# The first unit's maxima moved up, and the high parts of q and k stored from ScalarE's queue

## Chip, cores and metric

The kernel runs on one core of one Trainium2 chip. The metric is the device time of one execution in microseconds (us); lower is better.

## What is computed

The reference is a "macaron" layer on x of shape (8, 1024, 256): half a mixture-of-experts step, causal attention with 16 heads of 16, and again half a mixture-of-experts step.

```
x = x + 0.5 * ffn(layernorm(x))     # 8 experts, top 2, capacity 1.25 * N / 8
x = x + attn(layernorm(x))
x = x + 0.5 * ffn(layernorm(x))

attn: q, k, v = x @ Wq.T + bq, split(x @ Wkv.T + bkv)
      dots = causal(q * 16**-0.5 @ k.T);  out = softmax(dots) @ v @ Wo.T + bo
ffn:  probs = softmax(x @ gate_w.T); top 2 experts per token
      keep = counts <= cap     # an expert with more tokens than cap contributes nothing
```

An expert step adds something only where an expert's count stays within the capacity. The kernel computes the gates of both steps beside the attention, counts the tokens, and runs the expert part only if some expert is kept. In the profiled execution none is, so what is timed is the attention with the gates.

## The kernel before

Attention works through 8 batches of 1024 tokens; a batch has four units of four heads, 32 units in all (u = 4b + g). A unit has two streams of 18 tiles each on TensorE:

- **Maxima** (`m_steps`): tiles sm of scores q by k, causally masked, each reduced by VectorE to row maxima (`mx`). After the tiles of a half of the rows, `settle` joins them (`mxr`), makes the negative in a high and a low part (`mneg`), transposes it (`mside`) and has `send` write it to DRAM (`rows`) and read it back in another layout (`neg`).
- **Exponents** (`e_steps`): tiles sc, which begin with the negated maxima taken from `neg` by a matmul with the constant `take_m`; ScalarE takes the exponential (`pT`), GpSimd masks it where the diagonal crosses, and TensorE multiplies it with the values (`pav`).

Both streams share three pairs of PSUM banks: tile n needs the pair of tile n - 3, which its reader (VectorE for sm, ScalarE for sc) must have finished. The stream of maxima runs one unit ahead of that of exponents. Between these tiles, after every third, `gap` takes steps of other work from the queue `work`, at a pace `rate`: for the next batch the transposes (`enter`, pta to xnT), the projections (`project`, pq), the values (`values_of`, pv), and for the last batch the output projection (`leave`, px). Small pieces of VectorE's and GpSimd's work come from the queue `side` (`prepare` and `normed` for the layer norms, `gate_first` for the first step's gates, `biased_late` for adding the output bias to x). `start` sets off sequences of transfers with lags counted in tiles (`fetch`, `send`, `divide`).

`project` makes q and k of eight heads for 512 tokens at a time, eight steps per batch. ScalarE moves the product from PSUM (`whole`), casts it (`high`), and GpSimd takes the difference (`low`); four DMAs of 256 KB store the two parts to DRAM tile `parts`, for q in the order high, low, high, low and for k high, high, low, low. `fetch` reads them back as `qk` with heads along the partitions. Every engine's order is that of the source: each instruction is tied to the one before it on its engine. All these transfers are issued by SyncE (SP); ScalarE issues only loads at the start.

Before the loop over units stands the start: loads, the norm of batch 0 (`prepare_first`, `normed`), weights (`weights`, a generator called `turning`, whose last product is pt_b), projection of the first eight heads, the values of batch 0, the norm of batch 1, memsets and two `fetch`. Then, at u = -1, come the maxima of the first unit alone, and the loop. The profile gives most instructions the line of the helper that records them (L626), so tile names tell them apart.

Of the kernel before, what the change touches and what calls it, by code (L numbers as in the profile page):

```python
# [10 lines left out]
F32 = mybir.dt.float32  # L11
# [9 lines left out]
P = 128  # L21
# [8 lines left out]
def macaron_kernel(  # L30
# [16 lines left out]
    nc = tc.nc  # L47
# [81 lines left out]
                base=-(64 * h + k), channel_multiplier=1,  # L129
            )  # L130
    take_m = const.tile([P, P], F32R, name="take_m")
    nc.vector.tensor_copy(take_m, rows.to_broadcast([P, P]))

    wqT = const.tile([P, DC, D], F32, name="wqT")
    wkT = const.tile([P, DC, D], F32, name="wkT")
# [466 lines left out]
    def attention(run_no, src, dst, gate0, logits, tally):  # L602
# [4 lines left out]
        with stack:  # L607
# [76 lines left out]
            def normed(b, jj):  # L684
                mv, ve, rstd = lns[b]
                for j in (2 * jj, 2 * jj + 1):
                    xn = xns[b, j] = norm.tile([P, D], F32, tag="xn", name=f"xn_a{b}_{j}", bufs=4)
                    ln_apply(xn, xbs[b], j, mv, rstd[:, j : j + 1])
                    yield
                if b:  # L690
                    biased(b, jj)

            coming = {}
# [28 lines left out]
            def prepare_first():  # L722
                st, mv = ln_tiles("a0", "a")
                ve = norm.tile([P, TB], F32, tag="vea", name="ve_a0")
                rstd = norm.tile([P, TB], F32, tag="rstda", name="rstd_a0")
                lns[0] = (mv, ve, rstd)
                for n in (slice(0, TB // 2), slice(TB // 2, TB)):
                    for j in range(TB)[n]:
                        ln_stats(xbs[0], j, st, mv)
                    on.gpsimd.tensor_scalar(ve[:, n], mv[:, n, 1], EPS, None, ALU.add)  # L730
                    on.gpsimd.tensor_tensor(rstd[:, n], ve[:, n], half[:, n], ALU.pow)

            def enter(b):
                xnT = xnTs[b] = ap.tile([P, DC, S], F32, tag="xnT", name=f"xnT{b}", bufs=1)
# [22 lines left out]
            def project(b, gp):  # L757
                xnT = xnTs[b]
                parts = parts_d[b, gp] = passing.tile([2, 8, 4, HD, S], F32, tag=f"parts{gp}", name=f"parts{b}_{gp}")
                for s0 in range(0, S, 512):  # L760
                    for t, (wT, bT, scale) in enumerate(((wqT, bqT, QSCALE), (wkT, bkT, 1.0))):
                        pq = bank(f"pq{b}_{gp}_{s0}_{t}")
                        for o in (0, 256):
                            for c in range(DC):
                                product(
                                    pq[:, o : o + 256],
                                    wT[:, c, gp * P : (gp + 1) * P],
                                    xnT[:, c, s0 + o : s0 + o + 256],
                                    start=(c == 0),
                                    stop=(c == DC - 1),  # L770
                                )
                                if (c, o) != (DC - 1, 256):
                                    yield
                        whole = ap.tile([P, 512], F32, tag="whole", name=f"whole{b}_{gp}_{s0}_{t}")
                        high = ap.tile([P, 512], F32R, tag="high", name=f"high{b}_{gp}_{s0}_{t}", bufs=3)
                        low = ap.tile([P, 512], F32R, tag="low", name=f"low{b}_{gp}_{s0}_{t}", bufs=3)
                        on.scalar.activation(whole, pq, AF.Identity, bias=bT[:, gp : gp + 1], scale=scale)
                        on.scalar.copy(high, whole)
                        on.gpsimd.tensor_tensor(low.bitcast(F32), whole, high.bitcast(F32), ALU.subtract)
                        for c in range(4):  # L780
                            part = (high, low)[c // 2 if t else c % 2]
                            on.sync.dma_start(out=parts[t, :, c, :, s0 : s0 + 512], in_=part.bitcast(F32))
                        yield True


# [62 lines left out]
            def m_steps(u):  # L848
# [56 lines left out]
                def settle(hf):  # L905
                    mx = ap.tile([P, 4, 2, 2], F32, tag="mxr", name=f"mxr{u}_{hf}")
                    on.vector.tensor_reduce(
                        mx.rearrange("p x b a -> p x a b"),
                        mx_tiles[u % 3][hf].rearrange("p h r (a b) s -> p (h r) a b s", a=2),
                        AX.X,  # L910
                        ALU.max,
                    )
                    yield
                    mx = mx.rearrange("p x b a -> p x (b a)")
                    neg = ap.tile([P, 4, 2, 4], F32R, tag="mneg", name=f"mneg{u}_{hf}")
                    high, low = neg[:, :, 0], neg[:, :, 1]
                    on.vector.tensor_scalar(high, mx, -1.0, None, ALU.mult)
                    yield
                    on.vector.scalar_tensor_tensor(
                        low.bitcast(F32), mx, -1.0, high.bitcast(F32), ALU.mult, ALU.subtract  # L920
                    )
                    yield
                    turned = ap.tile([P, 32], F32, tag="mside", name=f"mside{u}_{hf}")
                    on.vector.transpose(turned, neg.bitcast(F32).rearrange("p x c i -> p (x c i)"))
                    start(send(hf, turned), 0)
                    yield

                def send(hf, turned):
                    rows = passing.tile([8, 512], F32, tag="rows", name=f"rows{u}_{hf}")
                    on.sync.dma_start(out=rows.rearrange("c (i s q) -> s c i q", i=4, s=4), in_=turned)  # L930
                    yield 6
                    for h in range(2):
                        on.sync.dma_start(
                            out=negs[u % 2][hf][64 * h : 64 * h + 2, :, :512].bitcast(F32),
                            in_=rows[4 * h : 4 * h + 4].rearrange("(r c) s -> c r s", c=2),
                        )
# [271 lines left out]
            next(turning, None)  # L1208
            next(turning, None)
            drain(read(1))  # L1210
            for t in (vaugs[0], *mx_tiles[0]):
                on.gpsimd.memset(t, 1.0 if t is vaugs[0] else -3.0e38)
            prepare_first()
            for jj in range(2):
                drain(normed(0, jj))
            next(turning, None)
            entering = enter(0)
            next(entering)
            next(entering)
            for jj in range(2, 4):  # L1220
                drain(normed(0, jj))
            projecting = project(0, 0)
            for _ in range(8):
                next(projecting)
            drain(fetch(0, 0, 512))
            drain(entering)
            drain(projecting)
            drain(fetch(0, 512, 512))
            drain(turning)
            drain(values_of(0))  # L1230
            drain(prepare(1))
            for t in (vaugs[1], *mx_tiles[1], *mx_tiles[2]):
                on.gpsimd.memset(t, 1.0 if t is vaugs[1] else -3.0e38)
            for pair_of in negs:
                for t in pair_of:
                    on.gpsimd.memset(t.bitcast(F32), 0.0)
            drain(fetch(1))

            work = deque([project(0, 1)])
            side += [biased_late(0), gate_first(0)]  # L1240
            timed = []
            behind = [0.0]
            last_on = []
# [41 lines left out]
            def maxima():  # L1285
                v, k = divmod(stream[0], 18)
                if v == NU:
                    return
                if k == 0:
                    units[v] = m_steps(v)  # L1290
                steps, settle, done = units[v]
                steps[k]()
                if k == max(done, 8) or k == 17:
                    side.appendleft(settle(int(k == 17)))
                    urgent[0] = 4
                if k == 17:
                    units.pop(v)
                stream[0] += 1

            for u in range(-1, NU):  # L1300
                b, g = divmod(u, NG)
                rate, every = 17 / 12, FILLS
                if u < 0:
                    pass
                elif g == 0:
                    spare[0] = False
                    if b + 1 < B:
# [1 line left out]
                        if b:  # L1309
                            work.append(mixed(leave(b - 1), project(b + 1, 1)))  # L1310
                        else:
                            work.append(project(b + 1, 1))
                        work.append(values_of(b + 1))
                    if b:
                        start(divide(b - 1, 1, 0), 4)
                        after[u - 1, 1] = divide(b - 1, 1, 1)
                        side.append(gate_first(b))
                elif g == 1 and b + 1 == B:
                    work.append(leave(b - 1))
                elif g == 2:  # L1320
                    if b == 0:
                        start(read(2), 40)
# [14 lines left out]
                    start(fetch(u + 2, lag=6), 8)  # L1337
                if u < 0:
                    for n in range(18):
                        step(maxima, 2, 4 if n < 5 else 4 / 3, 1)  # L1340
                else:
                    if u == 0:
                        for n in range(3):
# [86 lines left out]
```

## Time and profile before

| | |
|---|---|
| time, median of 3 runs | 1207.94 us (1207.55 to 1210.71) |
| the profiled execution: its time, its span | 1207.5 us, 1205.5 us |
| busy: PE, DVE, ACT, POOL | 1138.4, 935.2, 735.6, 433.8 us |
| exponentials `pT` | 576 of 1022 ns |
| reductions `mx` | 576 of 1215 ns |
| `high` casts | 64 of 619 ns (median) |
| stores of `parts`, high and low | 128 and 128 of 256 KB, all from SP |
| granted TensorE clock, mean | 0.978 |

PE is TensorE, DVE VectorE, ACT ScalarE, POOL GpSimd, SP SyncE; SPq and ACTq are the issuing of DMAs by these engines, which is not counted as busy time. The span is from the first to the last instruction; the time holds a little more.

### The profile page before, as it was taken

How to read it: one execution, taken by the hardware profiler on the slowest of the kernel's cores; microseconds unless marked ns; L12 is line 12 of the kernel's file. 1: busy time of each engine (PE TensorE's matmuls, PEld its weight loads, DVE VectorE, ACT ScalarE, POOL GpSimd, SP SyncE). 2: the span in 40 equal slices, each digit the busy share in tenths (PEclk: the TensorE clock that was granted, in tenths of full speed). 3: DMA queues.
4: the chain of work that ended last, by engine and by line, in shares of the span. 5: the costliest groups of instructions: out<-in, count | busy, mean ns of one | idle time of the engine just before them, and what ended most of it. 6: DMA issues, size and time to landing. Idle time of an engine off the chain costs nothing.

```text
span 1205.5 us, 36314 instructions
## 1 busy us (share of the span) xinstructions
PE 1138.4 (94%) x15178; PEld 663.1 (55%) x15178; DVE 935.2 (78%) x1652; ACT 735.6 (61%) x955; POOL 433.8 (36%) x772
## 2 busy tenths in 40 slices
PE   6789899999999999999999999999999999999983
PEld 4445555655556555655556555565556555555542
DVE  2687558887788877988788877888789888798834
ACT  3236656766666666665666656566666666665671
POOL 4633313543333423532235433333235322232331
PEclk9879999999999999999999999999999999999997
DMA  5644654354554646455563645546564555543211
GB/s 178 222 168 141 209 173 128 111 196 153 171 185 154 198 159 190 143 172 177 157 201 113 207 153 168 169 155 202 160 181 150 176 174 177 155 136 109 63 42 39
DMA packets 108517, 190.25 MB, mean 158 GB/s; under 512 B 24752, under 2 KB 42296, under 8 KB 108344
## 3 DMA queue, kind: packets, MB, share of 16 engines
q1 hardware_dynamic: 104952, 185.59, 47.8%
q8 instruction: 122, 2.00, 0.7%
q10 hardware_dynamic: 3392, 2.24, 0.6%
q14 instruction: 51, 0.42, 0.1%
HBM read 94.50 MB, written 93.31 MB: 156 GB/s over the span
## 4 chain that ended last, share of the span: by engine, by line
PE 76%; DVE 13%; DMA 5%; issue 1%; ACT 1%; POOL 1%; SPq 1%; POOLq 0%; ACTq 0%; DVEq 0%
PE sc L626 22%; PE pav L626 21%; PE sm L626 15%; PE pq L626 8%; DVE mx L626 8%; PE px L626 4%; PE pv L626 4%; PE pta L626 2%; DVE st_a L626 1%; DMA few<-sums 1%; DMA neg<-rows 1%; DMA rows<-mside 1%; SPq L626 1%; DVE mv_a L626 1%; DMA qk<-parts 1%
## 5 line engine op out<-in xcount | busy, mean ns | idle before, releaser
L626 DVE TENSOR_REDUCE mx<-sm 128x2 f32<-128x1024 f32 (+2 forms) x576 | 684.7, 1215 | 161.6 <-PE sm L626 159.9
L626 ACT ACTIVATE pT<-sc 128x1024 f32<-128x1024 f32 x576 | 573.0, 1022 | 309.6 <-PE sc L626 297.9
L626 PE MATMUL pav<-pT,vaug 128*32 128x256 f32 (+3 forms) x4608 | 329.7, 387 | 2.0 <-ACT att L626 1.4
L626 POOL TENSOR_SCALAR_AFFINE_SELECT pT<-pT 128x256 f32<-128x256 f32 (+1 forms) x448 | 191.0, 443 | 297.2 <-ACT pT L626 290.4
L626 PE MATMUL sm<-qk 64*128 64x512 f32 (+3 forms) x1536 | 266.2, 384 | 17.4 <-DVE mx L626 8.4
L626 PE MATMUL sc<-neg,take_m 64*128 64x512 f32 x1152 | 263.7, 454 | 16.6 <-DVE mx L626 8.9
L626 PE MATMUL sc<-qk 64*128 64x512 f32 (+3 forms) x1536 | 228.7, 334 | 0.0
L626 PEld LDWEIGHTS sm<-qk 64*128 64x128 f32 x1536 | 140.7, 187 | 120.4 <-issue 51.9
L626 POOL TENSOR_TENSOR low<-whole,high 128x512 f32<-128x512 f32 x64 | 82.0, 1282 | 311.3 <-ACT high L626 302.5
L626 PEld LDWEIGHTS pav<-pT,vaug 128*32 128x32 f32 x4608 | 113.7, 109 | 108.0 <-issue 52.2
L626 PEld LDWEIGHTS sc<-neg,take_m 64*128 64x128 f32 x1152 | 109.4, 186 | 106.8 <-issue 53.6
L626 PEld LDWEIGHTS sc<-qk 64*128 64x128 f32 x1536 | 146.2, 186 | 16.3
L626 PE MATMUL sm<-masked,before_k 64*128 64x128 bf16 (+1 forms) x1280 | 86.3, 213 | 0.0
L626 PE MATMUL pq<-xnT,wqT 128*32 128x256 f32 x1024 | 76.3, 391 | 0.5 <-ACT xnT L626 0.5
L626 PE MATMUL px<-woT,on 128*32 128x264 f32 x1024 | 76.5, 387 | 0.2 <-ACT on L626 0.2
L626 PE MATMUL pq<-xnT,wkT 128*32 128x256 f32 x1024 | 73.2, 395 | 0.0
L626 PE MATMUL pv<-wvT,xnT 128*32 128x264 f32 x1024 | 72.3, 390 | 0.0
L626 PEld LDWEIGHTS <-before_k 64*128 64x128 bf16 x1280 | 37.9, 96 | 43.1 <-issue 26.6
L626 POOL TENSOR_TENSOR x_a<-x_a,bo_all 128x512 f32<-128x512 f32 x32 | 41.6, 1304 | 28.1 <-DVE xn_a L626 28.1
L626 PEld LDWEIGHTS pq<-xnT,wqT 128*32 128x32 f32 x1024 | 34.0, 112 | 31.8 <-issue 13.9
L626 DVE TENSOR_TENSOR x_a<-px,x_a 128x256 f32<-128x256 f32 x64 | 26.2, 410 | 31.2 <-PE px L626 30.6
L626 PEld LDWEIGHTS px<-woT,on 128*32 128x32 f32 x1024 | 34.7, 110 | 26.6 <-issue 9.8
(131 smaller groups left out, 741.4 us busy)
## 6 DMA issues: line engine op xcount, KB each, us to landing
qk<-parts SPq DMA_DIRECT2D x124, 512.0 KB
parts<-high SPq DMA_DIRECT2D x128, 256.0 KB
parts<-low SPq DMA_DIRECT2D x128, 256.0 KB
sums<-att SPq DMA_DIRECT2D x62, 256.0 KB
out_dram<-x_a SPq DMA_DIRECT2D x16, 512.0 KB
on<-sums SPq DMA_DIRECT2D x30, 256.0 KB
rs<-inv SPq DMA_DIRECT2D x30, 256.0 KB
x_a<-in_L_attn_x_dram SPq DMA_DIRECT2D x13, 512.0 KB
```

Source lines behind the costliest of these rows:

```text
L626: i = call(*args, **kwargs)
```

## The change

Four things change. (1) In `project`, the DMAs of the high part are issued by ScalarE, behind the cast, in every batch; only the first store of q and of k in the whole kernel stays with SyncE. The low parts stay with SyncE. (2) For unit 0, `send` issues from ScalarE's queue, with other lags, and its first half is settled right after its fifth tile. (3) The start is put in another order: the norm of batch 0 is made in pieces of two, two and four tiles, the statistics of batch 1 come before the rest of the weights, and the values of batch 0 move from ahead of the loop into the work between the first unit's maxima; the gates and biases of batches 0 and 1 move into the loop. (4) In batch 0 the pace is 13/12 instead of 17/12, and the values of batch 1 are mixed with the second projection.

```
     prepare_first:
+        def some(j0, j1): ln_stats for j0..j1, then ve and rstd on GpSimd
+        memset vaugs[0], mx_tiles[0]
+        some(0, 2); some(2, 4)
+        drain(normed(0, 0)); next(turning, None); drain(normed(0, 1))
+        on.vector.tensor_copy(take_m, rows.to_broadcast([P, P]))
+        some(4, 8)
     project:
-        on.sync.dma_start(out=parts[t, :, c, :, s0 : s0 + 512], in_=part.bitcast(F32))
+        queue = on.scalar if part is high and (b or gp or s0 or c) else on.sync
+        queue.dma_start(out=parts[t, :, c, :, s0 : s0 + 512], in_=part.bitcast(F32))
     settle, send:
-        start(send(hf, turned), 0)
+        start(send(hf, turned), 0 if u else 2)
+        queue = on.sync if u else on.scalar      # rows and neg
-        yield 6
+        yield 6 if u else 4
     the start:
         projecting, fetch(0, 0, 512)
+        drain(normed(0, 2)), drain(normed(0, 3))
         drain(entering); drain(projecting); drain(fetch(0, 512, 512))
+        drain(fetch(1))
+        preparing = prepare(1); its first TB + 1 steps
+        memsets of negs, mx_tiles[1], mx_tiles[2], vaugs[1]
         drain(turning)
-        drain(values_of(0)); drain(prepare(1)); memsets; drain(fetch(1))
-        work = deque([project(0, 1)])
-        side += [biased_late(0), gate_first(0)]
+        work = deque([values_of(0), project(0, 1)])
+        side.append(preparing)
     maxima:
-        if k == max(done, 8) or k == 17:
+        if k == (max(done, 8) if v else done) or k == 17:
     the loop:
-        rate, every = 17 / 12, FILLS
+        rate, every = (17 if b else 13) / 12, FILLS
         g == 0, b == 0:
-            work.append(project(b + 1, 1)); work.append(values_of(b + 1))
+            work.append(mixed(values_of(b + 1), project(b + 1, 1)))
+            side.append(gate_first(0)); side.append(biased_late(0))
         g == 1, b == 0:
+            side.append(biased_late(1))
         u < 0:
-            step(maxima, 2, 4 if n < 5 else 4 / 3, 1)
+            step(maxima, 1, 16 / 5 if n < 5 else 16 / 13, 1)
```

More of the change, by code (lines that the diff above doesn't have):

```diff
@@ L131, in macaron_kernel @@
     take_m = const.tile([P, P], F32R, name="take_m")
-    nc.vector.tensor_copy(take_m, rows.to_broadcast([P, P]))
     wqT = const.tile([P, DC, D], F32, name="wqT")
@@ L689, in normed @@
                     yield
-                if b:
+                if b > 1:
                     biased(b, jj)
@@ L726, in prepare_first, with some @@
                 lns[0] = (mv, ve, rstd)
-                for n in (slice(0, TB // 2), slice(TB // 2, TB)):
-                    for j in range(TB)[n]:
+                def some(j0, j1):
+                    for j in range(j0, j1):
                         ln_stats(xbs[0], j, st, mv)
+                    n = slice(j0, j1)
                     on.gpsimd.tensor_scalar(ve[:, n], mv[:, n, 1], EPS, None, ALU.add)
                     on.gpsimd.tensor_tensor(rstd[:, n], ve[:, n], half[:, n], ALU.pow)
+                for t in (vaugs[0], *mx_tiles[0]):
+                    on.gpsimd.memset(t, 1.0 if t is vaugs[0] else -3.0e38)
+                some(0, 2)
+                some(2, 4)
+                drain(normed(0, 0))
+                next(turning, None)
+                drain(normed(0, 1))
+                on.vector.tensor_copy(take_m, rows.to_broadcast([P, P]))
+                some(4, 8)
             def enter(b):
@@ L924, in settle @@
                     on.vector.transpose(turned, neg.bitcast(F32).rearrange("p x c i -> p (x c i)"))
-                    start(send(hf, turned), 0)
+                    start(send(hf, turned), 0 if u else 2)
                     yield
                 def send(hf, turned):
+                    queue = on.sync if u else on.scalar
                     rows = passing.tile([8, 512], F32, tag="rows", name=f"rows{u}_{hf}")
-                    on.sync.dma_start(out=rows.rearrange("c (i s q) -> s c i q", i=4, s=4), in_=turned)
-                    yield 6
+                    queue.dma_start(out=rows.rearrange("c (i s q) -> s c i q", i=4, s=4), in_=turned)
+                    yield 6 if u else 4
                     for h in range(2):
-                        on.sync.dma_start(
+                        queue.dma_start(
                             out=negs[u % 2][hf][64 * h : 64 * h + 2, :, :512].bitcast(F32),
@@ L1210, in attention @@
             drain(read(1))
-            for t in (vaugs[0], *mx_tiles[0]):
-                on.gpsimd.memset(t, 1.0 if t is vaugs[0] else -3.0e38)
             prepare_first()
-            for jj in range(2):
-                drain(normed(0, jj))
-            next(turning, None)
             entering = enter(0)
@@ L1219, in attention @@
             next(entering)
-            for jj in range(2, 4):
-                drain(normed(0, jj))
             projecting = project(0, 0)
@@ L1225, in attention @@
             drain(fetch(0, 0, 512))
+            for jj in range(2, 4):
+                drain(normed(0, jj))
             drain(entering)
@@ L1228, in attention @@
             drain(fetch(0, 512, 512))
-            drain(turning)
[L1230 to L1237, printed above, removed]
-            work = deque([project(0, 1)])
-            side += [biased_late(0), gate_first(0)]
+            drain(fetch(1))
+            preparing = prepare(1)
+            for _ in range(TB + 1):
+                next(preparing)
+            for k in range(2):
+                for t in negs[k]:
+                    on.gpsimd.memset(t.bitcast(F32), 0.0)
+                for t in mx_tiles[k + 1]:
+                    on.gpsimd.memset(t, -3.0e38)
+            on.gpsimd.memset(vaugs[1], 1.0)
+            drain(turning)
+            work = deque([values_of(0), project(0, 1)])
+            side.append(preparing)
             timed = []
@@ L1311, in attention @@
                         else:
-                            work.append(project(b + 1, 1))
-                        work.append(values_of(b + 1))
+                            work.append(mixed(values_of(b + 1), project(b + 1, 1)))
+                        if b:
+                            work.append(values_of(b + 1))
                     if b:
@@ L1316, in attention @@
                         after[u - 1, 1] = divide(b - 1, 1, 1)
-                        side.append(gate_first(b))
+                    side.append(gate_first(b))
+                    if not b:
+                        side.append(biased_late(b))
                 elif g == 1 and b + 1 == B:
                     work.append(leave(b - 1))
+                elif g == 1 and b == 0:
+                    side.append(biased_late(1))
                 elif g == 2:
```

## The prediction

> **What bounds the kernel now.** I read the page first: its busy line and the chain that ended last.
>
> ```profile
> PE 1138.4 (94%) x15178; PEld 663.1 (55%) x15178; DVE 935.2 (78%) x1652; ACT 735.6 (61%) x955; POOL 433.8 (36%) x772
> PE 76%; DVE 13%; DMA 5%; issue 1%; ACT 1%; POOL 1%; SPq 1%; POOLq 0%; ACTq 0%; DVEq 0%
> ```
>
> TensorE is 94% busy and carries 76% of the chain; ScalarE carries 1%, so what it does now is nearly all covered. An average hides stages, so next come the stretches (length, busy time of PE, PEld, DVE, ACT, POOL, then granted clock, DMA share, GB/s):
>
> ```profile
> 34.00:46.20 12.20, 9.53 (x164) 5.05 (x156) 5.43 (x18) 4.83 (x18) 4.18 (x6) 1.00 0.61 211
> 46.20:76.50 30.30, 22.62 (x211) 10.26 (x211) 28.77 (x39) 4.75 (x8) 17.91 (x18) 0.72 0.60 217
> 147.00:153.00 6.00, 0.24 (x5) 0.16 (x2) 0.93 (x1) 1.02 (x1) 1.05 (x3) 0.72 0.50 178
> 261.00:406.00 145.00, 144.09 (x1987) 84.32 (x1980) 118.58 (x202) 95.37 (x125) 56.40 (x99) 1.00 0.54 171
> ```
>
> There are three regimes. Up to 76.5 us VectorE is the limit once its reductions begin (28.77 of 30.30 us). At 147 us everything stands still for 5.8 us. From 261 us on TensorE works 99% of the time, so each microsecond in which it waits is added to the total. The chain in order of time, before 77 us, gives the landmarks:
>
> ```profile
> 32.27 7.95 PE pv L626 x128
> 43.92 2.33 DVE xn_a L626 x4
> 46.24 1.14 DVE mx L626
> 71.36 4.99 DMA neg<-rows
> 76.49 0.84 PE sc L626 x4
> ```
>
> The value product of batch 0 is on the path for 8 us, then the normalising of batch 1; the first reduction starts at 46.2 and the first score tile at 76.5, after a DMA.
>
> **Part 1, the first unit's maxima move up (a gain).** In the changed order the maxima's first products follow pt_b directly, the value product is threaded between them, and VectorE's statistics of batch 1 come before it waits for pt_b.
> - pt_b ends at 32.27 now. ScalarE must also issue stores between its casts there. Two issues of 0.58 us each (row below) after the third cast push the next chain by about 1.2 us and the last pair adds as much, less the 0.78 us that this cast now waits for an older store: 1.8 us net. pt_b ends at 34.1 and the first reduction starts at 35.0, not 46.2.
> - The first five products (about 0.75 us each) now have all 16 value steps between them (128 matmuls took 7.95 us, so 0.45 to 0.5 each): 3.8 + 7.2 = 11 us, so the fifth reduction ends near 46. VectorE normalises three of batch 1's four tiles (0.64 us each) inside that.
> - Then the first half is settled (mxr, two mneg at 1.2 and mside: 2.8 us, as at 59.1 to 61.9 now), 13 reductions at 1.21 make 15.7, one tile 0.6, the second settling 1.2, one reduction of the next unit 1.2: 46 + 21.5 = 67.5. The score tile starts at 67.5 instead of 76.5: 9.0 us.
> - The gating of batch 0 (lc_f 1.17 us and some eight pieces of 0.2) leaves this stretch for the first attention unit, where VectorE is busy about 70%, and costs nothing there; without that cover it is some 4 us. The bias additions of batches 0 and 1 on GpSimd (8 of 1.3 us) go where it was busy 24 of 70 us: nothing. The memsets (neg 4.5 us for four, vaug 2.0) stay ahead of their first use.
> - The first unit's rows and neg copies go to ScalarE's queue. The second neg copy waits for the landing of rows (3.8 us after its issue ended, at 78.3 to 82.1 now), and behind it stands the second exp: 1.5 us back, between 0 and 3.
> Together 7.5 us gained. Bounds: 4 if the qk loads (now 42.95 to 52.3) arrive too late for the sixth product, 12 if PE's half clock (0.72 in the stretch) also goes.
>
> **Part 2, the standstill at 147 us (a gain).** The fourth qk load is issued at 143.28 behind a neg copy that waited 6.5 us for rows and behind four stores; TensorE stands before an sm until 152.87. The profile names no releaser there ("issue", 5.75 us); I infer this load, the only input of that tile still on its way. The pace of projection in batch 0 falls from 17/12 to 13/12, so the stores spread out, and half of them leave SP's queue. Between 0 and 8 us (5.8 and some half clock after it); I take 6, as later batches, with wider spacing, show no such wait.
>
> **Part 3, the high stores on ScalarE's queue (a loss).** Cost of one issue, from the tile view of high, and one place in the timeline:
>
> ```profile
> L626 SPq DMA_DIRECT2D parts<-high x128: 565/582/1683, 17.7 to 1029.7; - x128
> ```
> ```profile
> 253.90 0.69 ACT L626 ACTIVATE whole<-pq,bqT 128x512 f32<-128x512 f32 x1 [0.92 <-POOL pT L626]
> 254.04 0.40 PE L626 MATMUL sc<-neg,take_m 64*128 64x512 f32 x2
> 254.62 0.62 ACT L626 CAST high<-whole 128x512 fp32r<-128x512 f32 x1
> 255.15 2.18 ACT L626 ACTIVATE pT<-sc 128x1024 f32<-128x1024 f32 x2
> 256.22 0.56 PE L626 MATMUL sm<-qk 64*128 64x128 f32 x4
> ```
>
> Now the exp starts 0.1 us before the cast's end. With two stores in between, the queue waits for the cast (0.1 plus 0.02 to 0.07), issues twice (pairs take 1.23 us on SP) and starts the exp: 1.40 us later. Behind these issues stand the exps, and behind an exp stands TensorE: three PSUM pairs are shared by sm and sc, so the second sm after an sc needs that sc's exp done. Here sc (254.04) is read by the exp that ends at about 256.2 and sm starts at 256.22: no slack, so the whole 1.40 is lost. I read the slack so for the eight places of one batch (casts at 239.4, 245.5, 254.6, 262.5, 279.6, 294.1, 311.5, 328.1), letting ScalarE's idle time work the delay off and taking the worst exp of each. What is left over at 1.40 is 0.45, 0.47, 1.42, 0.47, 0.02, 0.64, 0.53, 0.21: 4.2 us. Six such batches make 25.3, the batch at 96 to 160 makes 4.4 in the same way: 29.7. The curve is steep: a delay of 1.0 leaves 11, 1.2 leaves 20, 1.6 leaves 41, 2.0 leaves 63. TensorE is idle some 11 of 839 us from 261 to 1100 for VectorE's sake and a little falls in there: I take 27.
>
> What SP gains for it: 126 issues of mean 0.65, but in the queue's own waits it stands most for ScalarE's cast (135.9 us, 48 times), that is, it has time; a qk load is waited for by sm only 1.9 us in all. No gain after batch 0.
>
> The Trainium skill, DMA: Bandwidth & Descriptors, section "Issuing engines are not separate DMA queues", speaks against the split: issuing from several engines saves only the sequencer's issue time, which is usually small beside the DMA. By it parts 2 and 3 would bring no transport at all, and the sum without part 2 would be 6 us longer. The trace agrees for the steady batches and leaves batch 0 open, where the pace, not the queue, is my reason.
>
> **The sum.** 27 - 7.5 - 6 = +13.5 us, against the profiled execution's 1207.5 us (span 1205.5 and 2.0 around it; the median is 0.4 higher): 1221, and I give 1220. With the ends of each part for a delay of 1.2 to 1.6 (17 to 38), the forecast's own range is 1209 to 1233.
>
> **The rivals.**
> - Faster: the issues find cover. The path is the exp behind the cast, at 56 places; it decides at a delay of about 1.1 us, below which the loss (under 15) is less than the 13.5 gained. For it: the chain has ScalarE at 1%, and ScalarE idles 470 us. Against it: the slack above is 0 to 1.5 us and the two shortest issues already take 1.13. At 1.0 it is 11 - 12 - 6 = -7: 1200. Chance 0.18.
> - Slower by far: an issue on ScalarE takes what SP's fourth of a burst takes (low stores reach a mean of 0.86 us and a maximum of 1.9), or its store waits for the landing of an older DMA on the other queue, which it now can. At a delay of 1.9 (57) less 13.5: 1251. For it: SP and ScalarE now issue at the same time. Against it: high stores come first in their burst and mostly take 0.58. Chance 0.12.
> - Part 1 and 2 bring little: the transfers set the start (217 GB/s in 46 to 76 us) and the standstill stays: 27 - 4 = +23: 1231. Chance 0.2. That the stores do not move is no rival: the built order shows each pair right behind its cast.
>
> **How the numbers follow.** The forecast has 0.5. No change within 0.3% (3.6 us, about what a measurement of this kernel can tell) needs loss and gain to meet: 0.10, taken from the forecast's and the first rival's edges. Below that lies most of the first rival, 0.17; above it the rest, 0.73. The range reaches into the first and the last two rivals: 1200 to 1242.
>
> **What would show it.** Right: the first mx near 35 us and the first sc near 67; no gap at 147; between high and the next pT some 1.2 us of ScalarE issuing; PE's waits for ACT pT grown by some 25 us, near 3 to 4 us in each later batch. Wrong: steady batches as long as before would refute part 3, a first sc after 73 part 1, a standstill in batch 0 part 2.

## The result, and the profile after

The changed kernel takes 1252.22 us (median of 6 runs, 1250.26 to 1256.01) against 1206.29 for the kernel before on the same chip: a ratio of 1.0386 (95% interval 1.0357 to 1.0415). The forecast was 1220, in a range of 1200 to 1242. The sign was right, the size was not. The profiled execution took 1251.04 us (span 1249.3), 43.5 more than the one of before, where 13.5 were forecast.

The page, busy line and chain that ended last:

```profile
PE 1153.4 (92%) x15178; PEld 662.0 (53%) x15178; DVE 944.6 (76%) x1652; ACT 737.0 (59%) x955; POOL 435.1 (35%) x774
PE 69%; DVE 9%; ACT 8%; DMA 6%; ACTq 4%; issue 2%; POOL 2%; SPq 0%; POOLq 0%; DVEq 0%
```

ScalarE is no busier than before (737.0 us against 735.6), but its work and its issuing (ACT and ACTq) have gone from 1% to 12% of the chain. The stretches, with the columns of before (length, busy time of PE, PEld, DVE, ACT, POOL, then granted clock, DMA share, GB/s):

```profile
34.00:46.20 12.20, 7.27 (x34) 6.30 (x38) 0.70 (x3) 1.66 (x6) 7.58 (x12) 0.50 0.63 197
46.20:76.50 30.30, 29.46 (x390) 13.42 (x382) 25.98 (x34) 8.75 (x24) 6.39 (x8) 0.95 0.51 177
147.00:153.00 6.00, 5.80 (x68) 3.38 (x70) 3.47 (x4) 4.12 (x6) 0.41 (x1) 1.00 0.67 222
261.00:406.00 145.00, 139.35 (x1900) 80.20 (x1896) 113.32 (x190) 91.29 (x117) 52.83 (x92) 0.99 0.51 160
```

From 34 to 46 us VectorE does almost nothing (0.70 us): the maxima that should have started at 35 are not there. At 147 us there is no standstill (5.80 of 6.00 us busy). From 261 us on TensorE loses 5.6 of 145 us, where it lost 0.9. The chain in order of time gives the new landmarks:

```profile
29.01 6.83 DMA qk<-parts
35.92 0.58 ACTq L625
36.54 1.87 ACTq L625
...
42.41 2.78 PE pt_b L625 x8
45.19 0.86 PE sm L625 x6
```

A qk load, issued by SP, is followed by two issues on ScalarE's queue, then by the products that end with pt_b, at 45.2 us (32.27 before, 34.1 forecast). The first maxima tile comes only then. What follows is seen in the timelines of PE and of ACT:

```profile
75.36 0.49 PE L625 MATMUL sc<-neg,take_m 64*128 64x512 f32 x2 [0.44 <-DVE mx L625]
79.78 0.54 ACTq L625 DMA_DIRECT2D rows<-mside  x1
80.36 0.59 ACT L625 COPY xnT<-pta 128x512 f32<-128x512 f32 x1 [5.88 <-DMA parts<-high]
```

The first score tile is 1.1 us earlier than before (76.49), but its exp is not: ScalarE stands for 5.88 us behind the last pair of stores and the copy to rows, which wait for older transfers. The first exp starts at 80.84, 5.5 us behind its tile (0.9 before).

A place in a later batch, timeline of all engines (start, length, engine, and in brackets the idle time before and its releaser):

```profile
400.73 0.62 ACT L625 CAST high<-whole 128x512 fp32r<-128x512 f32 x1
...
401.64 1.84 ACTq L625 DMA_DIRECT2D parts<-high  x2
...
403.53 1.94 ACT L625 ACTIVATE pT<-sc 128x1024 f32<-128x1024 f32 x2 [2.18 <-DMA qk<-parts]
404.61 0.64 PE L625 MATMUL pav<-pT,vaug 128*32 128x256 f32 x2 [2.32 <-ACT pT L625]
```

The exp starts 2.2 us behind the cast, and TensorE waits 2.32 us: not for a PSUM pair but in pav, for the exp's result. (It is one of six places at which the second store of the pair waits for a qk load as well.) The waits in sum (engine and tile, releaser: us in total, times, longest):

```profile
ACT pT L625 <- DMA parts<-high: 56.2, 43, 1.4
PE pav L625 <- ACT pT L625: 16.1, 7, 3.0
PE sc L625 <- ACT pT L625: 15.4, 29, 4.8
ACT pT L625 <- DMA qk<-parts: 13.9, 6, 2.9
PE sm L625 <- ACT pT L625: 4.7, 11, 0.6
```

Before, the waits of TensorE's products for pT came to 0.5 us. Now they are 36.2, and the largest row is pav, which no step of the prediction mentions. The waits of the kernel before had a sign of it, in the row of pav's weight load:

```profile
PEld pav L626 <- ACT pT L626: 6.7, 13, 0.5
```

At 13 places, two in each of batches 1 to 6, this load already stood waiting for the exp: there was no slack.

To see where the 43.5 us arise, I read the start of each unit's first exp from ScalarE's timeline (every 18th pT):

| stretch | before | after | difference | forecast |
|---|---|---|---|---|
| to the first exp of unit 0 | 77.35 | 80.84 | +3.5 | -9 |
| batch 0, first exp of unit 0 to that of unit 4 | 142.9 | 148.0 | +5.1 | -0.5 |
| batches 1 to 6, unit 4 to unit 28 | 839.0 | 874.8 | +35.7 | +23 |
| the rest, to the end of the time | 148.2 | 147.5 | -0.7 | 0 |

The forecast column is the sum of the prediction, spread over the stretches: 1.5 - 6 + 4 in batch 0, and 23 of the 27 of part 3 later. All three stretches missed in the same direction, by 12.5, 5.6 and 12.7 us.

### The profile page after: what moved, and what is told of

It is laid out like the page before. It is cut to its first block, busy times and chain, and to the rows that moved or that the text cites. A ratio compares the mean times of both kernels' runs of the same rounds, so it can differ in the third digit from the quotient of the medians.

```text
span 1249.3 us, 36304 instructions
## 1 busy us (share of the span) xinstructions
PE 1153.4 (92%) x15178; PEld 662.0 (53%) x15178; DVE 944.6 (76%) x1652; ACT 737.0 (59%) x955; POOL 435.1 (35%) x774
## 4 chain that ended last, share of the span: by engine, by line
PE 69%; DVE 9%; ACT 8%; DMA 6%; ACTq 4%; issue 2%; POOL 2%; SPq 0%; POOLq 0%; DVEq 0%
PE pav L625 20%; PE sc L625 19%; PE sm L625 13%; PE pq L625 7%; DVE mx L625 5%; PE pv L625 4%; ACTq L625 4%; ACT pT L625 4%; DMA qk<-parts 3%; PE px L625 3%; ACT whole L625 2%; PE pta L625 2%; ACT high L625 2%; DVE key_f L625 1%; DMA parts<-low 1%
## 5 line engine op out<-in xcount | busy, mean ns | idle before, releaser
L625 PE MATMUL sc<-neg,take_m 64*128 64x512 f32 x1152 | 267.2, 460 | 22.5 <-ACT pT L625 15.4
L625 PEld LDWEIGHTS sm<-qk 64*128 64x128 f32 x1536 | 139.8, 186 | 120.1 <-issue 46.5
L625 PE MATMUL pv<-wvT,xnT 128*32 128x264 f32 x1024 | 75.7, 393 | 0.0
L625 PEld LDWEIGHTS <-before_k 64*128 64x128 bf16 x1280 | 37.2, 95 | 41.8 <-issue 26.1
```

Source lines behind the costliest of these rows:

```text
L625: i = call(*args, **kwargs)
```

## The experiments

The first four separate the change into its parts. The two theories were: the late exp (the issues hold ScalarE, so exps and TensorE come late), and transport (stores in two queues, and queues that wait for each other). The measured differences stand against the median of the kernel before in the same comparison: 1206.45 for the first four, 1204.89 for the next four, 1206.63 for the last four.

**All stores back on SP, the rest of the change kept.**

```
-  queue = on.scalar if part is high and (b or gp or s0 or c) else on.sync
+  queue = on.sync
```

> The changed kernel with every store of parts issued by SyncE again. Theory A (the stores on ScalarE's queue are the whole loss, in the start too, and the new start is good): first sc near 67 to 70 us, batches 1 to 6 as long as before (139.8 us each), in all about 1195 to 1199 us. Theory B (the new order of the start is itself later): first sc at 77 us or later, in all 1206 to 1212.

Measured: 1209.74 us (1203.92 to 1214.33), ratio 1.0032 (1.0005 to 1.0060). So nearly all of the loss is the stores on ScalarE, and the new start order, by itself, gains nothing. The time is that of theory B, the first score tile (72.45) lies between the two. The trace tells why. pt_b ends at 30.9, 3.2 us earlier than forecast, but the first maxima tile then waits for qk, so the first reduction starts at 35.83; that 35.0 was forecast is luck. The fifth ends at 46.5, and the next tiles wait for qk again (timeline of PE in this kernel):

```profile
34.86 0.80 PE L625 MATMUL sm<-qk 64*128 64x512 f32 x2 [3.95 <-DMA qk<-parts]
...
54.27 0.79 PE L625 MATMUL sm<-qk 64*128 64x512 f32 x2 [4.10 <-DMA qk<-parts]
```

The maxima of the second half wait 2.0 and 4.1 us for qk. The first exp starts at 74.37, 3.0 us earlier than before, not 9. Unit 0 then lasts 42.0 us instead of 37.9, and unit 1, where the standstill was, 36.1 instead of 40.8: over batch 0 (143.0 us against 142.9) nothing is left of the gain.

**Only the stores of batch 0 on ScalarE.**

```
+  queue = on.scalar if part is high and not b and (gp or s0 or c) else on.sync
```

> The changed kernel with high stores on ScalarE's queue only in batch 0. Theory A: ScalarE again stands before its third and fourth pair of stores until older transfers have landed, first sc near 80 us as in the changed kernel, batches 1 to 6 as before: about 1206 to 1212 us, some 10 slower than the one with all stores on SyncE. Rival: the start's stores cost nothing, within 2 us of that one.

Measured: 1221.4 us (1215.83 to 1225.05), ratio 1.0131 (1.0069 to 1.0193), 11.7 more than with none. The first exp comes at 82.30, 7.9 later than with all on SP: the start is where these stores cost. Of the 7.9 us, 3.5 arise up to the first score tile (75.91) and the rest behind it, on ScalarE. The step of some 10 us was as expected, the time itself was not.

**The kernel before, with the high stores of batches 1 to 7 on ScalarE** (called the third kernel below).

```
-  on.sync.dma_start(...)
+  queue = on.scalar if part is high and b else on.sync
+  queue.dma_start(...)
```

> The kernel before with only the high stores of batches 1 to 7 moved to ScalarE's queue. Theory A: batches 1 to 6 each about 6 us longer, as in the changed kernel (35.7 together), batch 0 some 4 to 8 longer: 1243 to 1250 us. Rival (the new pace and side order lengthen the batches): within 10 us of before.

Measured: 1241.77 us (1235.9 to 1243.17), ratio 1.0293 (1.0233 to 1.0352): +35.3 us for 56 places, just below what was expected: batch 0 is not 4 to 8 us longer but 2.5 shorter, as its standstill is gone. The parts of the change nearly add up: 3.3 us (the new start), 11.7 (batch 0's stores) and 35.3 make 50.3, and the whole costs 45.9. The delay is what was forecast: cast end to next exp is 1.34 us in the median, -0.10 before, so 1.44 against 1.40. The loss is not. One place, timeline of all engines:

```profile
391.30 0.62 ACT L626 CAST high<-whole 128x512 fp32r<-128x512 f32 x1
...
391.94 1.23 ACTq L626 DMA_DIRECT2D parts<-high  x2
...
393.22 1.94 ACT L626 ACTIVATE pT<-sc 128x1024 f32<-128x1024 f32 x2 [1.31 <-DMA parts<-high]
394.30 0.41 PE L626 MATMUL pav<-pT,vaug 128*32 128x256 f32 x2 [1.45 <-ACT pT L626]
```

The full delay arrives in pav. Its wait for pT sums to 19.2 us in 13 places, one in batch 0 and two in each of batches 1 to 6. Before, only its weight load waited there, 0.5 us each.

**The kernel before, no store moved, ScalarE kept busy instead** (the fourth kernel). Two more casts behind `high` write a BF16 tile that nothing reads.

```
+  if b:
+      for k in range(2):
+          idle = ap.tile([P, 512], BF16, tag="idle", ...)
+          on.scalar.copy(idle, whole)
```

> The kernel before, all stores on SyncE, but behind each high cast of batches 1 to 7 two more casts into a tile that nobody reads, about 1.24 us of ScalarE, as long as the two issues. If the loss is the delay of the exps behind (occupancy): 4 to 5.5 us a batch, 1232 to 1242 us. If the loss comes from waits between the two queues or from transfers: under 10 us, below 1217.

Measured: 1227.67 us (1227.03 to 1233.37), ratio 1.0206 (1.0148 to 1.0264): +21.2 us for a delay of 1.18 us (exp 1.08 behind the cast), less than the 1232 to 1242 expected and far above 1217. No DMA changed its queue, and the same wait is there, in the waits view of this kernel:

```profile
PE pav L626 <- ACT pT L626: 15.7, 13, 1.2
```

So in the later batches the occupation of ScalarE alone makes such a loss, without any transport; whether it makes all of it, the longer casts below tell. That fits the section of the Trainium skill that the prediction weighed (DMA: Bandwidth & Descriptors, "Issuing engines are not separate DMA queues"), by which issuing from a second engine saves only the sequencer's time for the issue. No run here gained anything by it.

The next four ask which places cost, and whether queue or pace of unit 0 can mend the start.

**All stores on SP, and unit 0's rows and neg on SP with the old lags.**

```
-  start(send(hf, turned), 0 if u else 2)
-  queue = on.sync if u else on.scalar
-  yield 6 if u else 4
+  start(send(hf, turned), 0)
+  queue = on.sync
+  yield 6
```

> The new start with all stores on SyncE, and the first unit's rows and neg copies too on SyncE, with their old lags. If the second neg copy on ScalarE's queue (seven us before the second exp, in the run with all stores on SyncE) holds up the first attention unit, that unit is about 4 us shorter than its 42 us and the whole about 1204 to 1206 us. If SyncE is as late with them, or TensorE has other work meanwhile: 1208 to 1212.

Measured: 1209.3 us (1205.32 to 1215.51), ratio 1.0038 (1.0009 to 1.0067), as with all stores on SP. The first exp comes at 72.26, and unit 0 lasts 42.3 us again. Timeline of PE:

```profile
86.69 1.08 PE L625 MATMUL sc<-neg,take_m 64*128 64x512 f32 x2 [5.34 <-DMA neg<-rows]
```

The maxima of the second half reach neg late from either queue. With the stores alone on SP, the second exp waits 6.99 us on ScalarE behind the neg copies; with neg on SP too, the score tile waits 5.34 us for neg.

**The third kernel, without the second and the fifth step of each batch** (the two in which pav waits).

```
+  queue = on.scalar if part is high and b and (gp, s0, t) not in ((0, 0, 1), (1, 0, 0)) else on.sync
```

> The kernel before with the high stores of batches 1 to 7 on ScalarE's queue, but for two of the eight steps of a batch (the k step of the first 512 tokens and first eight heads, and the q step of the first 512 tokens and last eight heads), behind which the product with the values was seen to wait 1.4 us for its exp. By the slack at the PSUM pairs alone these two steps cost 0.5 us a batch: 1236 to 1240 us. If the product's own wait is the missing cost, 2.9 us a batch goes: 1219 to 1225.

Measured: 1219.49 us (1218.23 to 1221.23), ratio 1.0123 (1.0063 to 1.0183): +14.6 us, so two steps of eight make 20.7 of the 35.3. (In batches 1 to 6 the two profiled executions differ by 15.9 us; 2.1 us of their difference lie ahead of the first moved store and have nothing to do with it.) The prediction's slack gave these two 0.47 and 0.02 us a batch. pav's waits are gone; what is left of them is the row of the weight load that the kernel before has too:

```profile
PEld pav L626 <- ACT pT L626: 6.7, 13, 0.5
```

**The third kernel, one of the two stores of a step.**

```
+  queue = on.scalar if part is high and b and not c else on.sync
```

> The kernel before with one high store per step instead of two on ScalarE's queue in batches 1 to 7, so that the exp behind is about 0.8 us late instead of 1.44. By the slack at the PSUM pairs alone: 6 us in all, 1212. With the product's own waits (two a batch, without slack) 14 to 16 us: 1220 to 1223. Cost in proportion to the issues: half of 35, 1224.

Measured: 1217.17 us (1215.19 to 1221.48), ratio 1.0108 (1.0043 to 1.0173): +12.3 us for a delay of 0.79. Between the two theories, nearer to pav (its waits for pT are 10.4 us in the same 13 places, 0.8 each, again the whole delay).

**All stores and unit 0's transfers on SP, and the old pace in batch 0.**

```
-  rate, every = (17 if b else 13) / 12, FILLS
+  rate, every = 17 / 12, FILLS
```

> As the run with everything on SyncE, but with batch 0 at the old pace 17/12. If the slower pace took the standstill of batch 0 away, it is back: a gap of some 5 us in TensorE's work between 140 and 160 us and 4 to 8 us more in all than that run. If the standstill went with the new order of the start: the same within 2 us.

Measured: 1212.15 us (1210.56 to 1218.49), ratio 1.0066 (1.0035 to 1.0098). This is 2.9 us more than with the new pace, between the two expectations. Unit 1 lasts 36.8 us, and TensorE's only gap above 1.3 us between 76 and 200 us is a wait for neg at 85.7: the standstill does not return. The new pace, which part 2 gave as its reason, is not needed to remove it; whether the pace alone would do so was not tried. In the profiled executions unit 0 is 2.7 us longer (45.0 against 42.3); why stays open.

The last four test the two explanations that had come up by then.

**Only two early stores of the start on ScalarE** (one in each of the first two steps, all others on SP).

```
+  queue = on.scalar if part is high and not b and not gp and not s0 and c else on.sync
```

> The run with ScalarE's stores in batch 0 alone, but only the two of the first 512 tokens (one of q, one of k) stay on ScalarE's queue; the other stores are SyncE's. If ScalarE's waits before its third and fourth store pairs (until transfers of the other queue have landed) made the start late, pt_b ends near 31 us again instead of 46 and the whole is within 3 us of the run with all stores on SyncE, 1207 to 1212. If any store on ScalarE's queue costs it: 1215 to 1222.

Measured: 1210.06 us (1203.93 to 1212.92), ratio 1.0033 (1.0013 to 1.0052); the first exp at 72.80, pt_b at 30.2. These two are harmless. So it is the six pairs after them that cost the start. ScalarE's timeline in the changed kernel shows the first two:

```profile
23.14 0.62 ACT L625 CAST high<-whole 128x512 fp32r<-128x512 f32 x1
27.63 1.95 ACTq L625 DMA_DIRECT2D parts<-high  x2
...
30.41 0.62 ACT L625 CAST high<-whole 128x512 fp32r<-128x512 f32 x1
35.92 2.49 ACTq L625 DMA_DIRECT2D parts<-high  x2
38.45 0.17 ACT L625 COPY wvT<-pt_gate 128x16 f32<-128x16 f32 x1 [7.42 <-issue]
```

Each pair is held before its issue, for 3.9 us after the cast's end at 23.76 and for 4.9 us after 31.03, until older transfers have landed (the second until the qk load of SP, by the chain shown above); behind it stand ScalarE's copies of the weights, which pt_b needs. The last of the six stands ahead of the first exp, as shown with the result. What each pair costs was not separated.

**More casts, meant for the delay of the stores.** A third, shorter cast, `idle[:, :240]`, joins the two.

```
+          on.scalar.copy(idle[:, :240], whole[:, :240])
```

> The kernel before, all stores on SyncE, with ScalarE busy behind each high cast of batches 1 to 7 for as long as the stores held it (a third, shorter cast of 240 elements into the tile that nobody reads; the exp 1.44 us late instead of 1.18). If the loss of the moved stores in the later batches is nothing but this delay: batches 1 to 6 are 33 to 36 us longer in all, as with the stores, and the time is 1236 to 1242. If queue waits or transfers have a share, it stays below 1233.

Measured: 1249.35 us (1248.43 to 1250.28), ratio 1.0346 (1.0328 to 1.0365): +42.7 us. The casts took longer than intended: the exp starts 1.50 us behind `high`, a delay of 1.60 instead of 1.44. It is no equal of the stores, and lies above what was expected, but it brackets them: on a straight line between two casts (1.18 us, +21.2) and three (1.60 us, +42.7), the stores' delay of 1.44 would cost 34.5 us, an estimate, and the stores cost 35.3. So the delay accounts for nearly all of their loss.

**The third kernel, and the kernel before, with the product with the values due later.**

```
-  ready = count[0] + (5 if jb >= i else 3)
+  ready = count[0] + 5
```

On the third kernel:

> The kernel with the high stores of batches 1 to 7 on ScalarE's queue, with the products with the values taken at the earliest five tiles after their exp instead of three. If the product's wait for a late exp is the missing cost, its waits of 1.4 us go and the time falls by 10 to 20 us, to 1222 to 1232. If that room isn't there (six exp buffers, products taken when they are full), it stays within 4 us of 1242.

On the kernel before:

> The kernel before with the same later products: the other run's measure. Where no exp is late this should change nothing: 1203 to 1210 us. Shorter than 1203 would say that late exps cost the kernel before too.

Measured: 1235.71 us (1232.53 to 1239.19), ratio 1.0239 (1.0209 to 1.0270), for the third kernel, and 1207.48 (1203.43 to 1214.69), ratio 1.0008 (0.9982 to 1.0033), for the kernel before. pav no longer waits for pT in either, and the loss by the stores falls from 35.3 to 28.2 us: 7 less, and less than the 10 to 20 expected. The late exp then stops the tiles that need its PSUM pair: the waits of sc for pT are 11.7 us, against 4.4. With pav out of the way, the loss over batches 1 to 6 is 26.6 us (870.4 against 843.8), 4.4 a batch, where the prediction's slack gives 4.6 (table below).

## Why the prediction was wrong in size

The length of a batch, as the median over batches 1 to 6, sets the steps of part 3 against the measurements. Without added delay the median is 139.3 us for the kernel before, and 139.7 to 141.3 for the other kernels without late stores, so a difference of 1 us means little here: the pattern over the rows counts, not one of them.

| kernel | delay, us | median batch | loss a batch | by the prediction's slack |
|---|---|---|---|---|
| before | 0 | 139.3 | | |
| two extra casts | 1.18 | 143.9 | 4.6 | 2.7 |
| stores | 1.44 | 145.7 | 6.4 | 4.6 |
| three extra casts | 1.60 | 147.1 | 7.8 | 5.9 |
| one store | 0.79 | 142.6 | 3.3 | under 1.6 |
| stores at six places | 1.44 at six | 143.1 | 3.8 | 3.7 to 4.0 |

The last column is the prediction's curve (11, 20, 29.7 and 41 us for seven batches at 1.0, 1.2, 1.4 and 1.6), divided by seven and read between its points; for six places it is the listed leftovers at 1.40 without 0.47 and 0.02, and somewhat more at 1.44.

- **Part 3, the slack: the step that failed.** "The second sm after an sc needs that sc's exp done" was taken as the only way in which a late exp reaches TensorE. There is a second one: pav needs the exp's result, and at two of the eight places pav follows so closely that the whole delay, 1.47 us each (19.2 us over 13 places), becomes a wait. The prediction gave these places 0.49 us together; taking them out of the third kernel lowers the batch by 2.6 us. The wait follows the delay: 0.80, 1.21, 1.47 and 1.63 us a place at delays of 0.79, 1.18, 1.44 and 1.60. The other six cost 3.8, as forecast. The slope of the curve seems right as well: from 1.18 to 1.60 us the measured loss lies 1.8 to 1.9 above it, with one profiled execution for each. The term was too small by about 2 us a batch, of 6.4. The row of pav's weight load before would have told.
- **Part 3, the price of an issue** was right: 1.44 against 1.40 us. That TensorE would take up a little of it elsewhere (27 taken for 29.7) was not; of the 11 us of TensorE's idle time that it put down to VectorE, the waits of that stretch give VectorE 5.0.
- **Part 1, pt_b at 34.1: failed.** The prediction added two issues and their length, and nothing for a store that must wait for an older transfer before it is issued, though its second rival names exactly that wait. It happened in the start: by the trace's semaphores the two pairs waited for a store and a load of SP, which landed 9.2 and 6.8 us after their issue. pt_b ended at 45.2, and the first score tile came at 75.4, after the 73 that the prediction had named as its refutation. Yet of the 6.5 us by which the first exp is later than with all stores on SP, only 2.9 arise up to that tile, as that kernel waits for qk meanwhile; the other 3.6 arise behind it, where ScalarE's queue waits once more, a wait that the prediction did not have.
- **Part 1, the order itself: mis-sized.** With no store on ScalarE the reductions came near the forecast up to the fifth (35.83 for 35.0; 46.5 for 46), the first by luck. Then the bound "4 if the qk loads arrive too late for the sixth product" was what happened: 4.0 at the score tile, 3.0 at the exp, not 9. The return leg, 1.5 us for the second neg copy, was 4.1 to 4.4, by which unit 0 grew with all stores on SP; whether the gating that moved there has a share was not tried.
- **Part 2: right in size, wrong in reason, and not a gain.** The standstill is gone, and unit 1 is 4.9 us shorter in the changed kernel (35.9 against 40.8), but unit 0 is 5.9 longer (43.8 against 37.9). The old pace does not bring it back, and the third and fourth kernels, which leave batch 0's pace as it was, lose it as well (unit 1 36.9 and 36.4). It was no accident of one execution: the kernel before with the later products still stands for 3.6 us there. That TensorE waited for the fourth qk load was right: by the semaphores of the trace this load landed at 152.78, 0.1 us ahead of the tile, 9.5 us after its issue (6.9 in the changed kernel). What held the load stays open.
- **The rivals.** The one that ended near the result, 1251, was right in number only: a wait for an older DMA did decide the start, but in the later batches it touches one place in eight (6 waits, 13.9 us) and costs little: 35.7 us over batches 1 to 6 against 34.8 in the third kernel, in which no exp is put down to a qk load. Its delay of 1.9 us at every place was not there. "The transfers set the start" was right for the order alone: the kernel with all stores on SP waits for qk before its first maxima tile and between 47 and 55 us, and in unit 0 for neg. Whether fewer bytes in the start would give the 9 us was not tried.

No combination beat the kernel before; the nearest, with all or nearly all stores on SP, stand at +3 to +7 us.

## What to carry to other kernels

An engine that is 61% busy and 1% of the chain may have no free time at a given place. Here a DMA issue put behind one instruction delayed all that followed on that engine, so ask for every consumer of the delayed result (here the product that reads it, as well as the tile that reuses its buffer) how close behind it stands, and add up the closest. A store that moves to a compute engine's queue takes with it the wait for older transfers, and here this wait cost most at the start. Test such a move first by keeping the engine busy for the same time without any DMA.

## What the runs showed of the hardware

- A pair of 256 KB stores holds ScalarE's queue for 1.21 to 1.23 us at 51 of the third kernel's 56 places, about 0.59 us an issue. Longer holds in the changed kernel have two sources. At 401.64 us (1.84) both issues are short, and the second waits 0.66 us for a qk load. In the start (1.95 and 2.49) the second issue itself takes 1.33 and 1.87; why stays open. An issue of SP at the same time is not enough for that: with one store moved, 27 of 56 overlap with one, and their median is 0.59 us, against 0.58 for the others.
- A transfer of SP can hold a store of ScalarE: by the chain, the pair at 35.92 was released by the landing of a qk load that SP had issued at 29.01.
- A single late landing can lengthen a batch: batches 1 to 6 of the kernel before, with the same work in each, last from 138.2 to 142.1 us in one execution, and the longest of its units among those of one kind (37.2 against 34.5 us) holds a wait of 2.4 us for neg.
